# A spectral convolution loop regrouped: four turns a group, three PSUM bank pairs, split matrix halves

## The chip, the cores and the metric

The kernel runs on one core of a Trainium2 chip. The metric is the device time of one execution in microseconds (us). The kernel before has a median of 2602.63 us over three runs, from 2549.55 to 2603.58. All profile lines come from one profiled execution of 2596.2 us, whose span from first to last instruction is 2594.2 us.

## What is computed

Two layers act on x, four images of 56x56 positions with 128 channels, all in fp32. The first layer adds a 7x7 neighbourhood attention. The second adds a linear attention, and then a state-space layer (STU), which is the part that matters here:

```python
def _compute_spectral(u, sigma, phi, Mpp, Mpm):
    U_plus, U_minus = _stu_conv(phi, u, PADDED_SL)      # FFT convolution of u with 16 filters
    s = sigma ** SIGMA_POW
    out = jnp.einsum('btkd,k,kde->bte', U_plus, s, Mpp)
    out = out + jnp.einsum('btkd,k,kde->bte', U_minus, s, Mpm)
    return out

def _stu(u, sigma, phi, Mu, Mpp, Mpm):
    return _compute_spectral(u, sigma, phi, Mpp, Mpm) + _compute_ar_u(Mu, u)
...
for i, frac in enumerate((1, 2, 4, 8)):
    xi = x[:, :T // frac]
    si = _stu(xi, sigma, phi, M_u[i], M_phi_plus[i], M_phi_minus[i])
    outs.append(jnp.pad(si, ((0, 0), (0, T - si.shape[1]), (0, 0))))
y_soft = jax.nn.softmax((log_weights + gumbel) / TEMPERATURE)
y_hard = jax.nn.one_hot(jnp.argmax(y_soft), 4, dtype=y_soft.dtype)
weights = y_hard - jax.lax.stop_gradient(y_soft) + y_soft
return jnp.sum(jnp.stack(outs, axis=-1) * weights, axis=-1)
```

The convolutions are linear, so in frequency space each frequency has one complex 128x128 matrix, a sum over the 32 filters (16 plus, 16 minus), and the output there is that matrix times the transform of the tokens.

## The kernel before

**Stages.** A first stage selects and scales the filter matrices and transforms the filters (to about 100 us). Its `filter_matrices` (L277 on) sums the raw matrices with their weights into `to`, reorders them on GpSimd into `got` (L303), and brings them through DRAM to `mats`, which holds in each of four 32-partition strips one quarter of the output columns for the 32 filters. The main stage then runs both attentions image by image, to 1345 us. The spectral loop follows, to 2440 us. A last stage turns the result back into rows of the image, adds it, and writes the output.

**The spectral loop.** A frequency is m = m1 + 42 m2. The loop runs over 42 groups m1; each group has 56 points m2. Four kinds of work are done on TensorE for a group:

- `matrices` (L990) makes the 56 complex matrices of the group, 16 output columns of all of them in one call. It makes 16 matmuls, four columns by four strips, each with 32 rows, 128 columns of weights and 112 moving columns (56 points, two parts). They go to two PSUM tiles `pg` of two banks each. DVE copies the first tile and ACT the second to `gt` in SBUF (L1006). Eight calls make a group.
- `token_points` (L975) transforms the tokens of the group, one half of the image rows in one call, into the PSUM tile `pu`, from which DVE (L987) and ACT (L988) write `us`. `us` holds, for each point, 16 columns twice over: real and imaginary parts, and the negative imaginary part ahead of them, so that one slice serves each part of the complex product.
- `product` (L1011) multiplies one point: two matmuls, with 16 columns of `us` as weights and 128 columns of `gt` as moving data, that add up in PSUM. Point m2 writes 16 rows of one of the four 32-partition quadrants of `py`. After every 16 points `gather` (L1024) copies the used 16 rows of each quadrant to `ys`, two quadrants by ACT and two by DVE.
- `columns` (L1047) takes a group whose products have gone to DRAM and come back regrouped (`regroup`, L1033, `yd` to `yg`), transforms it along the points with two matmuls into `pz`, one tile of PSUM used twice, has ACT copy each to `zs` (L1059), and stores `zs` to `zd`.

Groups are pipelined: in step `it` the loop makes the matrices and token points of group `it`, the products of group `it`-1 and the columns of group `it`-3. TensorE's order is written out by hand (`manual_schedule` for PE, L1069). A step has eight turns. In each come one call of `matrices`, in turns 1 and 3 one of `token_points`, in turn 5 `columns`, and then seven points of `product`. The orders of the other engines are made by a scheduler.

**Buffers and waits.** [...] `pg` has two tags of one tile of two banks, so four banks and one buffer for each; `py` has two tiles of one bank; `pu` and `pz` one bank each. A tile's next user waits until the readers of its last content are done. When two engines read one PSUM tile, the framework also orders the second reader after the first. DMAs of the loop are issued on SyncE's queue: token loads `xm`, table loads `v`, `tok`, `back`, and `yd`, `yg`, `zd`.

Of the kernel before, what the change touches and what calls it, by code (L numbers as in the profile page):

```python
# [10 lines left out]
F32 = mybir.dt.float32  # L11
# [4 lines left out]
P = 128  # L16
B, H, W, C = 4, 56, 56, 128
# [33 lines left out]
NS, BR = 2, H // 2  # L51
N1, N2 = 42, W
NP = N1 * N2
NG = 4
# [3 lines left out]
NSB = NS * B  # L58
# [62 lines left out]
def hybrid_kernel(  # L121
# [23 lines left out]
    nc = tc.nc  # L145
# [17 lines left out]
    mats = keep.tile([P, GE, C], F32, name="mats")  # L163
# [15 lines left out]
    def evacuate(dst, src):  # L179

        flip[0] ^= 1
        if flip[0]:
            nc.scalar.copy(dst, src)
        else:
            nc.vector.tensor_copy(dst, src)
# [12 lines left out]
    with ExitStack() as ph:  # L198
# [78 lines left out]
        def filter_matrices():  # L277

            got = prep.tile([P, NG, GE, GE], F32, name="got")
            for c in range(4):  # L280
                cd = GE // 4
                to = prep2.tile([P, cd * C], F32, name="m_sum", bufs=1)
                for i in range(NE):
                    raw = prep2.tile([P, cd, C], F32, name="m_raw")
                    for s, m in enumerate((M_plus, M_minus)):
                        nc.sync.dma_start(
                            raw[64 * s : 64 * (s + 1)],
                            bass.AP(
                                m.tensor,
                                m.offset + (i * NF * C + c * cd) * C,  # L290
                                [[GE * C, NF * NG], [C, cd], [1, C]],
                            ),
                        )
                    src = raw.rearrange("p d e -> p (d e)")
                    if i == 0:
                        nc.vector.tensor_scalar(to, src, s_fac[:, 0:1], None, ALU.mult)
                    else:
                        nc.vector.scalar_tensor_tensor(
                            to, src, s_fac[:, i : i + 1], to, ALU.mult, ALU.add
                        )  # L300

                for g in range(NG):
                    nc.gpsimd.tensor_copy(  # L303
                        got[:, g, :, c * cd : (c + 1) * cd].rearrange("p (h i) d -> p h i d", i=4),
                        to.rearrange("p (d h g i) -> p g h i d", h=8, g=NG, i=4)[:, g],
                    )
            nc.sync.dma_start(wd, got.rearrange("p g e d -> p g (e d)"))
            for g in range(NG):
                for q in range(NG):
                    nc.sync.dma_start(  # L310
                        mats[32 * g : 32 * (g + 1), :, q * GE : (q + 1) * GE],
                        wd[:, g].rearrange("(k q) (e d) -> q k e d", q=NG, d=GE)[q],
                    )
# [60 lines left out]
    with main as ph:  # L374
# [552 lines left out]
        rows = iter(())  # L927
# [16 lines left out]
    with ExitStack() as ph:  # L944
        tabs = ph.enter_context(tc.tile_pool(name="tabs", bufs=2))
        sp = ph.enter_context(tc.tile_pool(name="sp", bufs=2))
        ps_g = ph.enter_context(tc.tile_pool(name="ps_g", bufs=1, space=bass.MemoryType.PSUM))
        ps_y = ph.enter_context(tc.tile_pool(name="ps_y", bufs=2, space=bass.MemoryType.PSUM))
        ps_x = ph.enter_context(tc.tile_pool(name="ps_x", bufs=1, space=bass.MemoryType.PSUM))

        chunk = {}

# [19 lines left out]
                nc.sync.dma_start(xm[part * N2 : (part + 1) * N2], xd[part * N1 + m1])  # L972
            return xm

        def token_points(m1, xm, us, s):  # L975

            pu = ps_x.tile([P, B, 2, N2], F32, tag="u", name="pu")
            for b in range(B):
                nc.tensor.matmul(  # L979
                    pu[:, b].rearrange("p c m -> p (c m)"),  # L980
                    xm[:, s, b, :],
                    tables_of(m1)[1],
                    start=True,
                    stop=True,
                )
            at = slice(s * B, (s + 1) * B)
            nc.vector.tensor_copy(us[:, 1:3, at, :], pu.rearrange("p b c m -> p c b m"))  # L987
            nc.scalar.mul(us[:, 0, at, :], pu[:, :, 1, :], -1.0)  # L988

        def matrices(m1, gt, eh):  # L990

            v = tables_of(m1)[0]
            pg = [ps_g.tile([P, 2, 512], F32, tag=f"g{q}", name=f"pg{q}") for q in range(2)]
            for i in range(4):
                for g in range(NG):
                    rows = slice(32 * g, 32 * (g + 1))
                    nc.tensor.matmul(  # L997
                        pg[g // 2][:, g % 2, 2 * N2 * i : 2 * N2 * (i + 1)],
                        mats[rows, 4 * eh + i, :],
                        v[rows],  # L1000
                        start=True,
                        stop=True,
                    )
            for q, copy in enumerate((nc.vector.tensor_copy, nc.scalar.copy)):
                e0 = 16 * eh + 8 * q
                copy(  # L1006
                    gt[:, :, e0 : e0 + 8, :].rearrange("p m (g i) c -> p g m i c", g=2),
                    pg[q][:, :, : 8 * N2].rearrange("p g (i m c) -> p g m i c", i=4, c=2),
                )

        def product(py, gt, us, m2):  # L1011

            j, slot = m2 % NG, m2 // NG % 4
            for c in range(2):

                nc.tensor.matmul(  # L1016
                    py[32 * j : 32 * j + 2 * NSB, slot, :],
                    us[:, 1 - c : 3 - c, :, m2],
                    gt[:, m2, :, c],
                    start=(c == 0),  # L1020
                    stop=(c == 1),
                )

        def gather(py, ys, q):  # L1024

            n = min(4, N2 // NG - 4 * q)
            for j in range(NG):
                rows = slice(32 * j, 32 * j + 2 * NSB)
                (nc.vector.tensor_copy if j % 2 else nc.scalar.copy)(  # L1029
                    ys[rows, 4 * q : 4 * q + n], py[rows, :n]  # L1030
                )

        def regroup(m1, ys):  # L1033
# [10 lines left out]
                )  # L1044
            return yg

        def columns(m1, yg):  # L1047

            zs = sp.tile([2 * N2, NS, B * C], F32, name="zs")
            for s in range(NS):  # L1050
                pz = ps_x.tile([2 * N2, B * C], F32, tag="z", name="pz")
                nc.tensor.matmul(  # L1052
                    pz,
                    tables_of(m1)[2],
                    yg[:, s * B : (s + 1) * B].rearrange("p k e -> p (k e)"),
                    start=True,
                    stop=True,
                )
                nc.scalar.copy(zs[:, s], pz)  # L1059
            for part in range(2):  # L1060
                nc.sync.dma_start(
                    zd[:, part * N1 + m1].rearrange("w s b e -> w (s b e)"),
                    zs[part * N2 : (part + 1) * N2].rearrange("w s f -> w (s f)"),
                )

        xms = {0: load_tokens(0)}
        gts, uss, ygs = {}, {}, {}
        LAG = 3
        with tc.manual_schedule(engines={mybir.EngineType.PE}):  # L1069
            for it in range(N1 + LAG):  # L1070
                ap = it - 1
                if it < N1:
                    gts[it] = sp.tile([P, N2, C, 2], F32, name="gt")
                    uss[it] = sp.tile([P, 3, NSB, N2], F32, name="us")
                    if it + 1 < N1:
                        xms[it + 1] = load_tokens(it + 1)
                if 0 <= ap < N1:
                    ys = sp.tile([P, N2 // NG, C], F32, name="ys")
                done = 0
                for eh in range(8):  # L1080
                    if it < N1:
                        matrices(it, gts[it], eh)
                        if eh in (1, 3):
                            token_points(it, xms[it], uss[it], eh // 2)
                    if eh == 5 and 0 <= it - LAG < N1:
                        columns(it - LAG, ygs.pop(it - LAG))
                    if 0 <= ap < N1:
                        for m2 in range(7 * eh, 7 * eh + 7):
                            if m2 % 16 == 0:
                                py = ps_y.tile([P, 4, C], F32, name="py")  # L1090
                            product(py, gts[ap], uss[ap], m2)
                            if m2 % 16 == 15 or m2 == N2 - 1:
                                gather(py, ys, m2 // 16)
                if 0 <= ap < N1:
                    ygs[ap] = regroup(ap, ys)
                xms.pop(it, None), gts.pop(ap, None), uss.pop(ap, None)


    with ExitStack() as ph:
# [91 lines left out]
```

## Time and profile before

| what | value |
|---|---|
| median of three runs | 2602.63 us |
| profiled execution, its span | 2596.2 us, 2594.2 us |
| mean granted TensorE clock | 0.791 |
| PE busy, of the span | 2149.8 us (83%) |
| DVE busy | 1348.2 us (52%) |
| ACT busy | 1077.8 us (42%) |
| first matmul of the spectral loop | 1350.0 us |
| last column product of the loop | 2438.8 us |

PE is TensorE's matmuls, PEld its weight loads, DVE is VectorE, ACT is ScalarE, POOL is GpSimd and SP is SyncE. In lines of the timeline come the start, the length, the engine, the line of the kernel, the operation, output<-inputs with their shapes, the number of instructions that were merged, and in brackets the engine's idle time before them and who ended it. An fp32 matmul leaves two records, so 16 matmuls show as x32. The granted clock is the share of TensorE's full speed that its throttle allowed.

### The profile page before, as it was taken

What the parts mean: (1) busy time and instruction counts of PE and PEld (TensorE: products, weight loads), DVE (VectorE), ACT (ScalarE), POOL (GpSimd) and SP (SyncE); (2) the same over time, 40 slices, a digit from 0 to 9 for tenths busy, and PEclk for the clock granted to TensorE, in tenths of its full rate; (3) what the DMA queues carried; (4) which work ended last, traced back from release to release, by engine and by line L of the source; (5) the groups of instructions that cost most, each with busy time, mean ns of one, the idle gap of its engine ahead of it and who ended that gap; (6) DMA issues with size and microseconds to landing.
All of it is one profiled execution on the core that took longest, in us unless ns stands there. A gap on an engine that the chain in (4) does not pass through costs nothing.

```text
span 2594.2 us, 66462 instructions
## 1 busy us (share of the span) xinstructions
PE 2149.8 (83%) x28564; PEld 1488.6 (57%) x28564; DVE 1348.2 (52%) x3324; ACT 1077.8 (42%) x2521; POOL 144.1 (6%) x287
## 2 busy tenths in 40 slices
PE   3069977898878987998868888888888888888498
PEld 3036655565645655665536766666676676666222
DVE  5246645464454645664425555556555555655132
ACT  0026542464334633564314555555555555555100
POOL 1110011001110002001000000000000000000000
PEclk8565588557975579656868999999999999999655
DMA  6631004011320113110351333433333343333597
GB/s 167 135 115 33 23 18 118 22 34 30 115 75 22 30 49 102 55 34 12 101 161 38 85 78 79 90 78 84 78 84 79 78 90 78 79 71 64 125 233 196
DMA packets 219512, 210.07 MB, mean 81 GB/s; under 512 B 43154, under 2 KB 187250, under 8 KB 218642
## 3 DMA queue, kind: packets, MB, share of 16 engines
q1 hardware_dynamic: 197850, 189.31, 29.2%
q10 hardware_dynamic: 21368, 16.51, 2.5%
q8 instruction: 224, 3.67, 0.6%
q14 instruction: 70, 0.57, 0.1%
HBM read 116.32 MB, written 89.45 MB: 79 GB/s over the span
## 4 chain that ended last, share of the span: by engine, by line
PE 56%; DVE 19%; ACT 10%; DMA 9%; issue 3%; POOL 1%; ACTq 1%; SPq 0%; DVEq 0%; POOLq 0%
PE pg L997 8%; PE pt L797 7%; PE sp L738 7%; DVE ys L1029 7%; PE py L1016 6%; ACT ys L1029 5%; DVE gt L1006 5%; PE po L819 4%; PE po L826 4%; ACT gt L1006 3%; PE bs L548 3%; PE pz L1052 2%; DMA out_dram<-tl 2%; PE pu L979 2%; PE po L1122 2%
## 5 line engine op out<-in xcount | busy, mean ns | idle before, releaser
L1006 DVE COPY gt<-pg 128x896 f32<-128x896 f32 x336 | 366.7, 1091 | 289.3 <-PE pg L997 278.1
L997 PE MATMUL pg<-v,mats 32*128 32x112 f32 x10752 | 398.0, 285 | 100.8 <-DVE gt L1006 83.9
L997 PEld LDWEIGHTS pg<-v,mats 32*128 32x128 f32 x10752 | 337.7, 190 | 190.1 <-DVE gt L1006 165.0
L1006 ACT COPY gt<-pg 128x896 f32<-128x896 f32 x336 | 304.5, 906 | 244.4 <-PE pg L997 232.4
L1016 PE MATMUL py<-gt,us 128*16 128x128 f32 x9408 | 389.8, 283 | 2.5 <-DVE gt L1006 1.6
L766 ACT ACTIVATE st<-st,nmx 96x252 f32<-96x252 f32 (+1 forms) x560 | 272.6, 488 | 190.5 <-DVE nmx L755 190.5
L1016 PEld LDWEIGHTS py<-gt,us 128*16 128x16 f32 x9408 | 295.0, 112 | 67.4 <-issue 31.1
L1029 DVE COPY ys<-py 16x512 f32<-16x512 f32 (+1 forms) x336 | 209.5, 624 | 160.3 <-ACT ys L1029 156.5
L755 DVE CUSTOM_DVE_ANT_0 st<-sp,relb 96x252 f32<-96x252 f32 (+1 forms) x560 | 203.5, 399 | 73.9 <-PE sp L738 73.5
L1029 ACT COPY ys<-py 16x512 f32<-16x512 f32 (+1 forms) x336 | 174.6, 520 | 149.3 <-DVE ys L1029 141.1
L738 PE MATMUL sp<-kp,qT 32*96 32x252 f32 (+1 forms) x1120 | 195.1, 635 | 30.4 <-DVE nmx L755 29.8
L797 PEld LDWEIGHTS pt<-ident,st 96*126 96x126 f32 (+1 forms) x1120 | 163.8, 216 | 87.4 <-issue 82.4
L797 PE MATMUL pt<-ident,st 96*126 96x96 f32 (+1 forms) x1120 | 201.5, 360 | 0.0
L1122 PE MATMUL po<-z,onto 84*56 84x512 f32 x224 | 125.8, 1066 | 21.1 <-DMA z<-zd 21.1
L1052 PE MATMUL pz<-yg,back 112*112 112x512 f32 x168 | 97.1, 660 | 46.7 <-ACT zs L1059 36.2
L597 ACT ACTIVATE hn<-acc,v 128x128 f32<-128x128 f32 (+1 forms) x208 | 83.0, 482 | 100.7 <-DVE v L588 99.4
L819 PE MATMUL po<-p,v_sb 126*32 126x96 f32 (+1 forms) x2240 | 115.1, 356 | 0.0
L738 PEld LDWEIGHTS sp<-kp,qT 32*96 32x96 f32 (+1 forms) x1120 | 67.3, 237 | 82.3 <-DVE nmx L755 58.4
L808 DVE COPY p<-pt 126x384 f32<-126x384 f32 (+1 forms) x140 | 74.1, 529 | 68.4 <-PE pt L797 64.0
L1131 DVE SCALAR_TENSOR_TENSOR tl<-po,hmask,tl 56x512 f32<-56x512 f32 x56 | 42.0, 750 | 124.3 <-PE po L1122 123.6
L766 ACT ACTIVATION_READ_ACCUMULATOR st<-st,nmx 96x1 f32 (+1 forms) x560 | 105.3, 188 | 0.0
L826 PE MATMUL po<-ident,wide 96*128 96x96 f32 x280 | 101.7, 465 | 0.0
(167 smaller groups left out, 2228.4 us busy)
## 6 DMA issues: line engine op xcount, KB each, us to landing
xd<-xs SPq DMA_DIRECT2D x112, 168.0 KB
xm<-xd SPq DMA_DIRECT2D x84, 224.0 KB
yd<-ys SPq DMA_DIRECT2D x168, 112.0 KB
yg<-yd SPq DMA_DIRECT2D x84, 224.0 KB
zd<-zs SPq DMA_DIRECT2D x84, 224.0 KB
z<-zd SPq DMA_DIRECT2D x14, 1344.0 KB
v_sb<-vpad SPq DMA_DIRECT2D x224, 63.0 KB
vpad<-vt SPq DMA_DIRECT2D x56, 112.0 KB
```

The source lines that it names most:

```text
L738: nc.tensor.matmul(t["sp"][h // 2][:nq, h % 2, : 2 * kn], qT[hs, ty, QR * x0 : QR * x0 + nq], kp[hs, y0 : y0 + KR, x0 : x0 + qc + KS - 1], ...
L755: nc.vector.tensor_tensor_reduce(st[:nq, h, : 2 * kn], t["sp"][h // 2][:nq, h % 2, : 2 * kn], relb[tiles[n][2]][:, h], -1.0, 3.0e38, ALU.a ...
L766: nc.scalar.activation(st[:nq, h, : 2 * kn], st[:nq, h, : 2 * kn], AF.Exp, bias=t["nmx"][:nq, h : h + 1], scale=-1.0, accum_out=t["sum"][: ...
L797: nc.tensor.transpose(pt[:kn, h, :nq], st[:nq, h, c * kn : (c + 1) * kn], ident[:nq, :nq])
L819: nc.tensor.matmul(po[hs, :nq], t["v"][:kn, c, hs], t["p"][c][:kn, h, :nq], start=(c == 0), stop=(c == 1),)
L826: nc.tensor.matmul(po[:, P : P + nq], t["wide"][:nq].rearrange("q h c -> q (h c)"), ident[:nq, :nq], start=True, stop=True,)
L997: nc.tensor.matmul(pg[g // 2][:, g % 2, 2 * N2 * i : 2 * N2 * (i + 1)], mats[rows, 4 * eh + i, :], v[rows], start=True, stop=True,)
L1006: copy(gt[:, :, e0 : e0 + 8, :].rearrange("p m (g i) c -> p g m i c", g=2), pg[q][:, :, : 8 * N2].rearrange("p g (i m c) -> p g m i c", i= ...
L1016: nc.tensor.matmul(py[32 * j : 32 * j + 2 * NSB, slot, :], us[:, 1 - c : 3 - c, :, m2], gt[:, m2, :, c], start=(c == 0), stop=(c == 1),)
L1029: (nc.vector.tensor_copy if j % 2 else nc.scalar.copy)(ys[rows, 4 * q : 4 * q + n], py[rows, :n])
L1052: nc.tensor.matmul(pz, tables_of(m1)[2], yg[:, s * B : (s + 1) * B].rearrange("p k e -> p (k e)"), start=True, stop=True,)
L1122: nc.tensor.matmul(po[64 * q : 64 * q + H].rearrange("p b c -> p (b c)"), onto[:, s], zin[q][:, i, s], start=(s == 0), stop=(s == NS - 1),)
```

## The change

The step keeps its work and its pipeline, and is divided otherwise.

- A step has four turns in place of eight. A turn makes two calls of `matrices`, then 16 points of `product` in a row (eight in the last turn), and one copy of the whole `py` tile to `ys`, by ACT and DVE in turn (`evacuate`). In the last turn both `token_points` and both `columns` stand between matrices and products.
- `ps_g` becomes one ring of three tiles of two banks. A call of `matrices` takes two of them. In each tile the first bank holds columns that DVE copies and the second columns that ACT copies, so four copies of 448 elements replace two of 896. `gt` is split in two halves of 64 columns, one written by each engine. `filter_matrices` orders the columns of `mats` to match.
- `py` has one bank. The token points and columns take their PSUM from one bank used twice (`x0`, `x1`) and from a tile of the ring (`xx`, a bank for each).
- `us` becomes two lasting tiles with two more blocks of 8 columns, zeroed once by GpSimd. A product's weights are then 32 columns wide, and fill the whole quadrant of `py`.
- The column products are copied by ACT and DVE in turn, each has its own PSUM, and their store is issued after `regroup`.

```diff
@@ filter_matrices
-                        got[:, g, :, c * cd : (c + 1) * cd].rearrange("p (h i) d -> p h i d", i=4),
-                        to.rearrange("p (d h g i) -> p g h i d", h=8, g=NG, i=4)[:, g],
+                        got[:, g, :, c * cd : (c + 1) * cd].rearrange("p (n i) d -> p n i d", i=4),
+                        to.rearrange("p (d h n q i) -> p q h n i d", h=2, n=8, q=2, i=4)[
+                            :, g // 2, g % 2
+                        ],
@@ pools
-        ps_g = ph.enter_context(tc.tile_pool(name="ps_g", bufs=1, space=bass.MemoryType.PSUM))
-        ps_y = ph.enter_context(tc.tile_pool(name="ps_y", bufs=2, space=bass.MemoryType.PSUM))
+        sp1 = ph.enter_context(tc.tile_pool(name="sp1", bufs=1))
+        ps_g = ph.enter_context(tc.tile_pool(name="ps_g", bufs=3, space=bass.MemoryType.PSUM))
+        ps_y = ph.enter_context(tc.tile_pool(name="ps_y", bufs=1, space=bass.MemoryType.PSUM))
...
+        us2 = [sp1.tile([P, 5, NSB, N2], F32, name=f"us{i}") for i in range(2)]
+        for t in us2:
+            nc.gpsimd.memset(t[:, 3:], 0.0)
@@ matrices
-            pg = [ps_g.tile([P, 2, 512], F32, tag=f"g{q}", name=f"pg{q}") for q in range(2)]
+            pg = [ps_g.tile([P, 2, 512], F32, tag="g", name="pg") for q in range(2)]
...
-            for q, copy in enumerate((nc.vector.tensor_copy, nc.scalar.copy)):
-                e0 = 16 * eh + 8 * q
-                copy(
-                    gt[:, :, e0 : e0 + 8, :].rearrange("p m (g i) c -> p g m i c", g=2),
-                    pg[q][:, :, : 8 * N2].rearrange("p g (i m c) -> p g m i c", i=4, c=2),
-                )
+            for q in range(2):
+                for h, copy in enumerate((nc.vector.tensor_copy, nc.scalar.copy)):
+                    e0 = 8 * n + 4 * q
+                    copy(
+                        gt[:, h, :, e0 : e0 + 4, :],
+                        pg[q][:, h, : 8 * N2].rearrange("p (i m c) -> p m i c", i=4, c=2),
+                    )
@@ product
-                    py[32 * j : 32 * j + 2 * NSB, slot, :],
-                    us[:, 1 - c : 3 - c, :, m2],
-                    gt[:, m2, :, c],
+                    py[32 * j : 32 * (j + 1), slot, :],
+                    us.rearrange("p c k m -> p (c k) m")[:, NSB * (1 - c) : NSB * (5 - c), m2],
+                    gt[:, :, m2, :, c],
@@ columns
-                pz = ps_x.tile([2 * N2, B * C], F32, tag="z", name="pz")
...
-                nc.scalar.copy(zs[:, s], pz)
+            evacuate(zs[:, s], pz)
@@ the loop
-                for eh in range(8):
+                for q in range(4):
                     if it < N1:
-                        matrices(it, gts[it], eh)
-                        if eh in (1, 3):
-                            token_points(it, xms[it], uss[it], eh // 2)
-                    if eh == 5 and 0 <= it - LAG < N1:
-                        columns(it - LAG, ygs.pop(it - LAG))
+                        matrices(it, gts[it], 2 * q)
+                        matrices(it, gts[it], 2 * q + 1)
+                    if q == 3:
+                        x0 = ps_x.tile([P, 512], F32, tag="x", name="px")
+                        xx = ps_g.tile([P, 2, 512], F32, tag="g", name="xx")
+                        x1 = ps_x.tile([P, 512], F32, tag="x", name="px")
+                        if it < N1:
+                            token_points(it, xms[it], us2[it % 2], 0, x0)
+                            token_points(it, xms[it], us2[it % 2], 1, xx[:, 0])
+                        if 0 <= az < N1:
+                            columns(az, ygs[az], zs, 0, xx[:, 1])
+                            columns(az, ygs[az], zs, 1, x1)
                     if 0 <= ap < N1:
-                        for m2 in range(7 * eh, 7 * eh + 7):
-                            if m2 % 16 == 0:
-                                py = ps_y.tile([P, 4, C], F32, name="py")
-                            product(py, gts[ap], uss[ap], m2)
-                            if m2 % 16 == 15 or m2 == N2 - 1:
-                                gather(py, ys, m2 // 16)
+                        n = min(16, N2 - 16 * q)
+                        py = ps_y.tile([P, 4, C], F32, name="py")
+                        for m2 in range(16 * q, 16 * q + n):
+                            product(py, gts[ap], us2[ap % 2], m2)
+                        evacuate(ys[:, 4 * q : 4 * q + n // NG], py[:, : n // NG])
                 if 0 <= ap < N1:
                     ygs[ap] = regroup(ap, ys)
+                if 0 <= az < N1:
+                    store_columns(az, zs)
+                    ygs.pop(az)
```

More of the change, by code (lines that the diff above doesn't have):

```diff
@@ L973, in load_tokens, with token_points @@
             return xm
-        def token_points(m1, xm, us, s):
-            pu = ps_x.tile([P, B, 2, N2], F32, tag="u", name="pu")
+        def token_points(m1, xm, us, s, pu):
+            pu = pu[:, : 2 * B * N2].rearrange("p (b c m) -> p b c m", b=B, c=2)
             for b in range(B):
@@ L988, in token_points, with matrices @@
             nc.scalar.mul(us[:, 0, at, :], pu[:, :, 1, :], -1.0)
-        def matrices(m1, gt, eh):
+        def matrices(m1, gt, n):
             v = tables_of(m1)[0]
-            pg = [ps_g.tile([P, 2, 512], F32, tag=f"g{q}", name=f"pg{q}") for q in range(2)]
+            pg = [ps_g.tile([P, 2, 512], F32, tag="g", name="pg") for q in range(2)]
             for i in range(4):
@@ L998, in matrices @@
                         pg[g // 2][:, g % 2, 2 * N2 * i : 2 * N2 * (i + 1)],
-                        mats[rows, 4 * eh + i, :],
+                        mats[rows, 4 * n + i, :],
                         v[rows],
@@ L1016, in product @@
                 nc.tensor.matmul(
-                    py[32 * j : 32 * j + 2 * NSB, slot, :],
-                    us[:, 1 - c : 3 - c, :, m2],
-                    gt[:, m2, :, c],
+                    py[32 * j : 32 * (j + 1), slot, :],
+                    us.rearrange("p c k m -> p (c k) m")[:, NSB * (1 - c) : NSB * (5 - c), m2],
+                    gt[:, :, m2, :, c],
                     start=(c == 0),
                     stop=(c == 1),
[L1022 to L1030, printed above, removed]
                 )
@@ L1045, in regroup, with columns, store_columns @@
             return yg
-        def columns(m1, yg):
-            zs = sp.tile([2 * N2, NS, B * C], F32, name="zs")
-            for s in range(NS):
-                pz = ps_x.tile([2 * N2, B * C], F32, tag="z", name="pz")
[L1052 to L1059, printed above, removed]
+        def columns(m1, yg, zs, s, pz):
+            pz = pz[: 2 * N2]
+            nc.tensor.matmul(
+                pz,
+                tables_of(m1)[2],
+                yg[:, s * B : (s + 1) * B].rearrange("p k e -> p (k e)"),
+                start=True,
+                stop=True,
+            )
+            evacuate(zs[:, s], pz)
+        def store_columns(m1, zs):
             for part in range(2):
@@ L1066, in hybrid_kernel @@
         xms = {0: load_tokens(0)}
-        gts, uss, ygs = {}, {}, {}
+        gts, ygs = {}, {}
         LAG = 3
@@ L1070, in hybrid_kernel @@
             for it in range(N1 + LAG):
-                ap = it - 1
+                ap, az = it - 1, it - LAG
                 if it < N1:
-                    gts[it] = sp.tile([P, N2, C, 2], F32, name="gt")
-                    uss[it] = sp.tile([P, 3, NSB, N2], F32, name="us")
+                    gts[it] = sp.tile([P, 2, N2, C // 2, 2], F32, name="gt")
                     if it + 1 < N1:
@@ L1078, in hybrid_kernel @@
                     ys = sp.tile([P, N2 // NG, C], F32, name="ys")
-                done = 0
-                for eh in range(8):
+                if 0 <= az < N1:
+                    zs = sp.tile([2 * N2, NS, B * C], F32, name="zs")
+                for q in range(4):
                     if it < N1:
-                        matrices(it, gts[it], eh)
-                        if eh in (1, 3):
-                            token_points(it, xms[it], uss[it], eh // 2)
-                    if eh == 5 and 0 <= it - LAG < N1:
-                        columns(it - LAG, ygs.pop(it - LAG))
-                    if 0 <= ap < N1:
-                        for m2 in range(7 * eh, 7 * eh + 7):
-                            if m2 % 16 == 0:
-                                py = ps_y.tile([P, 4, C], F32, name="py")
-                            product(py, gts[ap], uss[ap], m2)
-                            if m2 % 16 == 15 or m2 == N2 - 1:
-                                gather(py, ys, m2 // 16)
+                        matrices(it, gts[it], 2 * q)
[10 more added lines that the diff above has]
+                            columns(az, ygs[az], zs, 1, x1)
+                    if 0 <= ap < N1:
+                        n = min(16, N2 - 16 * q)
[3 more added lines that the diff above has]
+                        evacuate(ys[:, 4 * q : 4 * q + n // NG], py[:, : n // NG])
@@ L1094, in hybrid_kernel @@
                 if 0 <= ap < N1:
                     ygs[ap] = regroup(ap, ys)
-                xms.pop(it, None), gts.pop(ap, None), uss.pop(ap, None)
+                if 0 <= az < N1:
+                    store_columns(az, zs)
+                    ygs.pop(az)
+                xms.pop(it, None), gts.pop(ap, None)
     with ExitStack() as ph:
```

## The prediction

> **What bounds the kernel now.** I read the granted clock and the busy time by stretches first, to find the stage that the change touches. The spectral loop fills the middle of the page: its first matrices start at 1350 us and its last column product at 2438 us. Between 1400 and 2400 us each 200 us look alike, at clock 1.00:
>
> ```profile
> 1800.00:2000.00 200.00, 176.01 (x3967) 137.61 (x3964) 118.06 (x144) 102.31 (x160) 0.00 (x0) 1.00 0.36 81
> ```
>
> (stretch, then busy time and count of PE, PEld, DVE, ACT, POOL, then clock, DMA share, GB/s). PE is busy 88%, DVE 59%, ACT 51%, DMA a third: TensorE with its waits is the bound, and the copies matter where they make it wait. The waits in the loop say where:
>
> ```profile
> PEld pg L997 <- DVE gt L1006: 152.8, 240, 1.8
> DVE ys L1029 <- ACT ys L1029: 147.1, 278, 0.6
> PE pg L997 <- DVE gt L1006: 75.3, 121, 1.5
> PEld pz L1052 <- ACT zs L1059: 65.2, 38, 1.7
> ```
>
> (who waited for whom, us, times, longest). Matrices wait for the copy that frees their only pair of banks; that copy is late because it queues behind gathers of `ys`, which alternate between DVE and ACT, each waiting for the other. One group's length comes from the column products, one set a group: the first starts at 1441.4 us (group 3), the one of group 41 at 2398.16, so 956.76/38 = 25.18 us a group.
>
> The timeline inside a group gives the pieces (start, length, engine, line, work, idle before it and who ended it):
>
> ```profile
> 1807.59 1.15 PE L979 MATMUL pu<-tok,xm 112*128 112x112 f32 x8
> ...
> 1808.66 1.15 PE L1016 MATMUL py<-gt,us 128*16 128x128 f32 x28
> 1808.77 0.62 DVE L987 COPY us<-pu 128x448 f32<-128x448 f32 x1
> 1809.42 0.36 ACT L988 ACTIVATE us<-pu 128x224 f32<-128x224 f32 x1 [0.77 <-DVE us L987]
> ...
> 1809.74 1.16 PE L997 MATMUL pg<-v,mats 32*128 32x112 f32 x32
> ...
> 1810.83 1.17 PE L1016 MATMUL py<-gt,us 128*16 128x128 f32 x28
> 1810.94 1.09 DVE L1006 COPY gt<-pg 128x896 f32<-128x896 f32 x1 [1.55 <-PE pg L997]
> 1811.00 0.91 ACT L1006 COPY gt<-pg 128x896 f32<-128x896 f32 x1 [1.22 <-PE pg L997]
> ...
> 1812.08 0.98 PEld L997 LDWEIGHTS pg<-v,mats 32*128 32x128 f32 x32 [0.36 <-DVE gt L1006]
> ```
>
> Three readings. Matrices take 1.09 us from their start to the next work's start, and their copy starts 1.20 after their start. DVE ends a copy at 1812.03 and PE goes on at 1812.08: 0.05. And `us` shows what happens when both engines read one PSUM tile: ACT waits for DVE although another part is read, and starts 0.03 after it; the two copies of `gt`, from two tiles, run side by side.
>
> **What the Trainium skill says.** "PSUM — Partial Sum Buffer", Specifications: ScalarE and VectorE can read PSUM in parallel at full rate as long as they don't collide in a bank. The `gt` copies agree (1091 and 906 ns, together); so an order between them on two banks is the program's, not the chip's. "TensorEngine Tiling (Array Packing)", Key Properties: changing the tiling mode drains the array. Here 28 product records have their loads issued in 0.88 us, but 1.08 pass before the next matrices where nothing is waited for, so about 0.2 to 0.27 a switch. "TensorE: Matmul & The Clock Gate", Part 1: the clock falls after an idle window of some 3.4 us. No run shows that number by itself; the trace keeps 1.00 in stretches of 3.4 us with PE busy for only 1.9. Same page, LDWEIGHTS: the load's time goes with its columns. The trace bounds that for the wider weights, below.
>
> **The change, part by part**, with group times in us.
>
> *Gathers.* Per group 16 copies of 16 partitions (684 and 574 ns, the last four 417 and 356) become four copies of 128 partitions with the same length. About 9.0 us of alternating copies go, and 3x0.63+0.39, about 2.3, remain. None is on PE's path afterwards: each runs during the next turn's first matrices, which need 1.20 before their own copy can start. The price without that cover is 0.7 a turn.
>
> *Products.* `us` grows to 32 columns of weights for full quadrants. In the attention, loads of 126x32 have a shortest time of 106 ns and those of 128x16 a median of 108; I take no difference. Bounds: none below, since the moving columns stay the same; above, an estimate from the skill's price on that page (columns/1.2 ns): 16 more columns are 13 ns, over four quadrants 3.3 a record, 224 records 0.75 a group. The pace is read where products run in a row at the loop's end:
>
> ```profile
> 2408.46 4.04 PE L1016 MATMUL py<-gt,us 128*16 128x128 f32 x128 [1.58 <-DVE gt L1006]
> ```
>
> (4.04-0.27)/128 = 29.4 ns a record. Sixteen points are 64 records: 1.89+0.27 = 2.16; eight are 1.21.
>
> *Matrix copies.* This part decides. Each pair tile now holds one half for DVE and one for ACT. In the built program every ACT copy of `gt` waits for a DVE count only, none for PE: it follows the DVE copy of its own tile, as `us` does in the profile. PE in its turn waits for the ACT count of the copy that frees a pair. A copy has 448 elements: DVE 0.62 (the `us` row has that size), ACT between 0.36 for 256 and 0.57 for 512, so 0.52. Totals per group rise from 8x1.09 to 16x0.62 = 9.9 on DVE and from 7.2 to 8.3 on ACT, far from full.
>
> *The ring.* A turn writes four pair tiles from a ring of three: A takes a0, a1; B takes b0, b1; b1 lands on a0's buffer. PE is in order, so all of B but four records, and the 16 products queued behind B, wait for a0's copies. From A's start: 1.20 to DVE's start, 0.62, hand-over 0.03, ACT 0.52, back to PE 0.06: B resumes at 2.43. B's rest is 1.09-0.10 = 0.99: 3.42. Products 2.16: 5.58. The next turn's A finds its buffers free (b0's ACT copy ends about 4.7 us into the turn). So three turns are 16.74. Without the wait A and B would take about 1.9 of it; the stall costs 1.5 a turn.
>
> *Last turn.* 3.42, then both token points in a row: 16 records, 0.89+1.09 = 1.98: 5.40. The column product into `xx` waits for ACT's read of the other half of `xx` (its wait is on that count): 0.11+0.62+0.03+0.36+0.06 = 1.18: 6.58. Two columns, 0.86+1.05: 8.49 (the profile's 1.11 a pair, 0.25 of it drain, and 1.04 to the next products). Eight points: 9.70. Before, the second column product waited for ACT instead (0.88); its own tile now removes that.
>
> *Sum.* 16.74+9.70 = 26.44 against 25.18: +1.26 a group, 42 groups: +53. The first group, at half clock and without products, stalls as before but with its token points no longer filling waits: +4. The tail has one gather in place of four: about -4. Two memsets on POOL before the loop have no row here; their first reader is the products some 30 us later, so 0. The pool copies of the filter matrices keep their sizes: 0. DMAs keep sizes and count; on SP's queue a store of `zd` now stands between those of `yd`, with a whole group of slack. Against the profiled execution of 2596.2: 2649. The median of the runs shown is 6.4 above that: 2655, or +2.0%.
>
> **Rivals.** (1) *Copies side by side* (not slower). If the halves of a tile were read together, B would resume at 1.20+0.62+0.06 = 1.88, 0.55 earlier in each of four turns: 24.2 a group, -41 us, 2562. It decides at the hand-over in each tile: the loss is gone once a turn's stall shortens by 0.31. For it: different banks; against it: the waits as built, and `us` in this trace. The same place, smaller, gives no measurable change when the chain is shorter by some tenths. (2) *The stall hides wholly*, as three pairs might promise: 19.2 of PE's own work and the 1.18 of `us`: 20.4 a group, -200, 2400. Against it: PE is in order and no product stands between A and B. (3) *The clock falls*: an idle 1.3 in each turn lets the gate close at times. At half clock A, B and sixteen points take 2.1, 1.9 and 3.9, a turn 9.2 and a group some 44; one group in twenty at that pace adds 2.1x17.6 = 37, so 2692; a tenth 2729. For it: group 0 of the profile stays at 0.50 with PE busy 2.06 in 3.24 us. Against it: the loop holds 1.00 with 1.9 in 3.4, and a turn of the new loop has about 2.1 in its worst 3.4. (4) *Wider loads cost* 0.75 a group: +31, 2686.
>
> **Numbers.** Main case, with (4) as its upper edge: 0.84, a range of 2625 to 2686, which lies on both sides of the 2% line (2654.7) that is about what a measurement of this kernel can tell from no change. Side by side: 0.05. Hidden wholly: 0.03. Clock: 0.08. Runs of the kernel before go from 2549.55 to 2603.58, from a cause that this profile doesn't show; with a part of that below and the clock case above the range is 2605 to 2695. Slower by over 2%: half of the main case with the clock: 0.50. Within 2%: 0.47, the other half and the copies side by side. Faster: 0.03.
>
> **What would show it.** Right: a group of 26.4 us; PE waiting at matrices for ACT's `gt` about 1.3 us four times a group; DVE-to-ACT hand-overs on every `gt`; ACT copies of 0.52; products of 64 records in 2.16; `ys` off the list of waits; clock 1.00. Wrong: `gt` copies of one tile starting together, PE's wait at B under 1 us, product records over 31 ns, or a clock below 1.00 in the loop.

## The result and the profile after

The changed kernel takes 2677.4 us, median of four runs (2675.1 to 2679.69): slower, with a ratio of 1.0489 to the kernel before, interval 1.0463 to 1.0515. The forecast was slower, 2655 us, +2.0%. The profiled execution takes 2675.1 against 2596.2, which is 79 us or 3.0%. Of the 95 executions of all kernels here, seven, of four kernels, came some 50 us below the others of the same kernel, from a cause that no run shows, and the ratio above compares 2677 with two such executions of the kernel before (2549.55 and 2555.49). In the fifth experiment below the medians are 2677.13 to 2604.43, 1.028.

Ahead of the loop little moved: its first matrices start at 1351.1 us, before at 1350.0. From there to the last column product it is 1164.7 us, before 1088.8: +75.9. The stretch of the loop that the prediction showed, here from 1400 to 2400 us, of the changed kernel (busy time and count of PE, PEld, DVE, ACT, POOL, then clock, DMA share, GB/s):

```profile
1400.00:2400.00 1000.00, 798.45 (x18496) 678.55 (x18500) 454.15 (x776) 404.06 (x777) 0.00 (x0) 1.00 0.34 74
```

PE fell to 80% busy, DVE to 45%, ACT to 40%, the clock stayed at 1.00. Every engine waits more. The waits in the same stretch (us in total, times, longest):

```profile
ACT gt L1017 <- DVE gt L1017: 441.7, 297, 2.7
...
PEld pg L1007 <- ACT gt L1017: 187.8, 149, 1.6
PE pg L1007 <- ACT gt L1017: 161.4, 149, 1.4
...
PEld xx L1052 <- ACT us L997: 47.0, 35, 1.3
```

The waits of gathers for each other are gone. In their place ACT's copy of `gt` waits for DVE's, and matrices wait for ACT. The count is four a group, and the mean of one wait is 1.26 us (187.8/149), where a wait for DVE's copy took 0.64 before (152.8/240). One turn of the timeline:

```profile
1814.35 1.37 PE L1007 MATMUL pg<-v,mats 32*128 32x112 f32 x36
...
1815.54 1.16 DVE L1017 COPY gt<-pg 128x448 f32<-128x448 f32 x2 [2.36 <-PE pg L1007]
...
1816.20 1.06 ACT L1017 COPY gt<-pg 128x448 f32<-128x448 f32 x2 [1.16 <-DVE gt L1017]
...
1816.79 1.15 PE L1007 MATMUL pg<-v,mats 32*128 32x112 f32 x28 [1.07 <-ACT gt L1017]
...
1817.86 2.30 PE L1027 MATMUL py<-gt,us 128*32 128x128 f32 x64
...
1820.09 1.37 PE L1007 MATMUL pg<-v,mats 32*128 32x112 f32 x36
```

The first row is A's 32 records and four of B's, merged; then PE stands until ACT has finished the first of its two copies, 2.44 us after A's start. The turn takes 5.74. The last turn of a group has a second stall, between its token points and its columns:

```profile
1802.24 1.15 PE L988 MATMUL px<-tok,xm 112*128 112x112 f32 x8
...
1805.04 0.36 ACT L997 ACTIVATE us<-xx 128x224 f32<-128x224 f32 x1 [0.54 <-DVE us L996]
...
1805.45 1.11 PE L1052 MATMUL xx<-yg,back 112*112 112x512 f32 x2 [1.17 <-ACT us L997]
...
1807.35 1.25 PE L1027 MATMUL py<-gt,us 128*32 128x128 f32 x32
```

From the first token point to the products it takes 5.11 us, of which PE stands 1.17 until ACT has read the other half of `xx`. Column products show the group, `xx` at 1452.72 us and again at 2295.57, 31 groups later: 27.19 us in the mean (one of the 31 took 28.8, the others 27.1 to 27.2), before 25.18.

The products' weight loads before and after, and the copies of `ys` after, from the lists of groups (busy, mean ns of one, idle before and its releaser):

```profile
L1016 PEld LDWEIGHTS py<-gt,us 128*16 128x16 f32 x9408 | 295.0, 112 | 67.4 <-issue 31.1
...
L1027 PEld LDWEIGHTS py<-gt,us 128*32 128x32 f32 x9408 | 304.3, 144 | 47.5 <-issue 31.3
...
L185 DVE COPY ys<-py 128x512 f32<-128x512 f32 x84 | 46.9, 558 | 114.7 <-PE py L1027 109.3
```

A load of 32 columns takes 144 ns in the mean where the one of 16 took 112. The 558 ns of DVE's copies of `ys` is a mean over two sizes. No engine waits for a copy of `ys` in the stretch from 1400 to 2400 us any more.

### The profile page after: what moved, and what is told of

Its sections match the earlier page's. It is cut to its first block, busy times and chain, and to the rows that moved or that the text cites. A ratio compares the mean times of both kernels' runs of the same rounds, so it can differ in the third digit from the quotient of the medians.

```text
span 2673.4 us, 66713 instructions
## 1 busy us (share of the span) xinstructions
PE 2132.3 (80%) x28564; PEld 1533.1 (57%) x28564; DVE 1240.7 (46%) x3450; ACT 995.7 (37%) x2563; POOL 146.0 (5%) x289
## 4 chain that ended last, share of the span: by engine, by line
PE 72%; DVE 11%; DMA 7%; ACT 5%; issue 2%; POOL 1%; ACTq 1%; SPq 0%; DVEq 0%; POOLq 0%
PE pg L1007 14%; PE py L1027 12%; PE pt L799 7%; PE sp L740 7%; DVE gt L1017 4%; PE po L821 4%; ACT gt L1017 3%; PE po L828 3%; PE bs L550 3%; PE po L1133 2%; PE xx L1052 2%; PE px L988 2%; DMA z<-zd 2%; PE bs L883 1%; PE xx L988 1%
## 5 line engine op out<-in xcount | busy, mean ns | idle before, releaser
L1017 DVE COPY gt<-pg 128x448 f32<-128x448 f32 x672 | 388.3, 619 | 439.0 <-PE pg L1007 439.0
L1007 PE MATMUL pg<-v,mats 32*128 32x112 f32 x10752 | 432.0, 286 | 189.7 <-ACT gt L1017 183.6
L1017 ACT COPY gt<-pg 128x448 f32<-128x448 f32 x672 | 355.4, 533 | 510.8 <-DVE gt L1017 510.8
L1007 PEld LDWEIGHTS pg<-v,mats 32*128 32x128 f32 x10752 | 371.6, 190 | 251.8 <-ACT gt L1017 214.6
L1027 PE MATMUL py<-gt,us 128*32 128x128 f32 x9408 | 346.4, 291 | 2.1 <-DVE ys L185 1.3
L1027 PEld LDWEIGHTS py<-gt,us 128*32 128x32 f32 x9408 | 304.3, 144 | 47.5 <-issue 31.3
L1133 PE MATMUL po<-z,onto 84*56 84x512 f32 x224 | 126.9, 1067 | 21.8 <-DMA z<-zd 21.8
L185 DVE COPY ys<-py 128x512 f32<-128x512 f32 x84 | 46.9, 558 | 114.7 <-PE py L1027 109.3
L1133 PEld LDWEIGHTS po<-z,onto 84*56 84x56 f32 x224 | 32.5, 207 | 116.2 <-issue 101.0
L1052 PE MATMUL xx<-yg,back 112*112 112x512 f32 x84 | 48.5, 660 | 54.1 <-ACT us L997 45.5
```

Source lines behind the costliest of these rows:

```text
L1007: nc.tensor.matmul(pg[g // 2][:, g % 2, 2 * N2 * i : 2 * N2 * (i + 1)], mats[rows, 4 * n + i, :], v[rows], start=True, stop=True,)
L1017: copy(gt[:, h, :, e0 : e0 + 4, :], pg[q][:, h, : 8 * N2].rearrange("p (i m c) -> p m i c", i=4, c=2),)
L1027: nc.tensor.matmul(py[32 * j : 32 * (j + 1), slot, :], us.rearrange("p c k m -> p (c k) m")[:, NSB * (1 - c) : NSB * (5 - c), m2], gt[:, : ...
L1052: nc.tensor.matmul(pz, tables_of(m1)[2], yg[:, s * B : (s + 1) * B].rearrange("p k e -> p (k e)"), start=True, stop=True,)
L1133: nc.tensor.matmul(po[64 * q : 64 * q + H].rearrange("p b c -> p (b c)"), onto[:, s], zin[q][:, i, s], start=(s == 0), stop=(s == NS - 1),)
```

## The experiments

The theory is that two engines read each pair of banks one after the other, and that PE stands until the first pair is free again, because the fourth pair tile of a turn lands on its buffer. Its rivals are wider loads, the throughput of the copying engines, and a time that lies elsewhere in the kernel.

**The kernel before again.** No edit.

> The kernel before, unchanged, profiled a second time. The two profiled executions differ by 79 us (2596.2 to 2675.1), the compared runs by 4.9%, some 125 us: 46 us are not in the profile that the forecast was made from. Theory A: the loop of the kernel before can run at a shorter group than the 25.18 us of that profile (24.1 would give 46 us over 42 groups). Theory B: the time lies ahead of the loop, whose first matrices then start near 1305 us in place of 1350. If this execution takes 2596 again, it tells neither.

Measured: 2603.73 us over 18 runs (2598.26 to 2612.65); its profiled execution takes 2598.26 (2596.2 in the profile that the forecast started from), the first matrices start at 1354.6 us, and the group is 25.18 again. So that profile was a fair one. Neither theory is shown: none of the 18 executions came near 2552, and neither did any profiled one, so where those 50 us lie stays open.

**One tile for each copy.** The pair tile is cut into two tiles of one bank; each is read by one engine.

```diff
-        ps_g = ph.enter_context(tc.tile_pool(name="ps_g", bufs=3, space=bass.MemoryType.PSUM))
+        ps_g = ph.enter_context(tc.tile_pool(name="ps_g", bufs=6, space=bass.MemoryType.PSUM))
...
-            pg = [ps_g.tile([P, 2, 512], F32, tag="g", name="pg") for q in range(2)]
+            pg = [ps_g.tile([P, 512], F32, tag="g", name="pg") for g in range(NG)]
...
-                        pg[g // 2][:, g % 2, 2 * N2 * i : 2 * N2 * (i + 1)],
+                        pg[g][:, 2 * N2 * i : 2 * N2 * (i + 1)],
...
-                        pg[q][:, h, : 8 * N2].rearrange("p (i m c) -> p m i c", i=4, c=2),
+                        pg[2 * q + h][:, : 8 * N2].rearrange("p (i m c) -> p m i c", i=4, c=2),
...
-                        xx = ps_g.tile([P, 2, 512], F32, tag="g", name="xx")
+                        xx = [ps_g.tile([P, 512], F32, tag="g", name="xx") for h in range(2)]
...
```

> The changed kernel with a PSUM tile of one bank for each copy (a ring of six in place of three pairs), so that DVE's copy and ACT's copy of one call of matrices no longer read one tile. Theory (serial copies in the pair): PE resumes at matrices B 1.88 us after A's start in place of 2.44, 0.55 less in each of four turns, and the wait of the column product for ACT's read of us (1.2) goes with the split of xx: 27.1 - 2.2 - 1.2 = 23.7 us a group, about 2530 us. Rival (the copies' order costs nothing, PE waits for the engines' throughput): group stays within 0.5 of 27.1, 2655 to 2675.

Measured: 2520.4 us, median of four runs (2472.12 to 2525.05, three of them from 2518 on); the group is 23.42 (1469.27 to 2288.98 us, 35 groups). A turn of it:

```profile
1805.25 1.37 PE L1007 MATMUL pg<-v,mats 32*128 32x112 f32 x36
...
1806.43 1.16 DVE L1017 COPY gt<-pg 128x448 f32<-128x448 f32 x2 [2.33 <-PE pg L1007]
1806.47 0.97 ACT L1017 COPY gt<-pg 128x448 f32<-128x448 f32 x2 [0.52 <-PE pg L1007]
1807.11 0.97 PEld L1007 LDWEIGHTS pg<-v,mats 32*128 32x128 f32 x28 [0.66 <-DVE gt L1017]
```

The two engines copy side by side from two tiles, and PE resumes 1.86 us after A's start in place of 2.44. In the last turn the column product no longer waits for the read of `us`: from the first token point to the products it takes 3.69 us in place of 5.11. Four times 0.58 and once 1.42 are 3.74 of the 3.77 us by which the group is shorter. The time is gone where the theory puts it, and the order of the two readers is what made it: the copies are as many and as long as in the changed kernel (620 and 537 ns, there 619 and 533).

**Products between the two calls of matrices.** The pair tiles stay.

```diff
                         matrices(it, gts[it], 2 * q)
+                    if 0 <= ap < N1:
+                        n = min(16, N2 - 16 * q)
+                        py = ps_y.tile([P, 4, C], F32, name="py")
+                        for m2 in range(16 * q, 16 * q + 8):
+                            product(py, gts[ap], us2[ap % 2], m2)
+                    if it < N1:
                         matrices(it, gts[it], 2 * q + 1)
...
-                        for m2 in range(16 * q, 16 * q + n):
+                        for m2 in range(16 * q + 8, 16 * q + n):
                             product(py, gts[ap], us2[ap % 2], m2)
```

> The changed kernel with eight of a turn's sixteen products moved between its two calls of matrices; pair tiles and copies as they are. Theory (PE is in order and nothing stands between A and B): the 1.3 us wait at B is covered by 1.25 us of products; a turn is 1.09+1.25+1.09+1.25 and some 0.2 of waits at b1 and a1, 4.9 in place of 5.75, the last turn 8.5 in place of 9.8: 23.2 us a group, about 2510 us. Rival (the wider copies and loads are what costs): no more than 0.3 a group gained, about 2660.

Measured: 2503.65 us (2502.11 to 2506.84), ratio to the kernel before 0.9609, interval 0.9584 to 0.9634; group 23.00. From its waits and timeline:

```profile
PEld pg L1007 <- ACT gt L1017: 21.8, 111, 1.8
```

```profile
1814.76 1.15 DVE L1017 COPY gt<-pg 128x448 f32<-128x448 f32 x2 [1.25 <-PE pg L1007]
...
1815.47 1.01 ACT L1017 COPY gt<-pg 128x448 f32<-128x448 f32 x2 [1.17 <-DVE gt L1017]
1815.84 1.18 PEld L1007 LDWEIGHTS pg<-v,mats 32*128 32x128 f32 x32 [0.18 <-issue]
```

ACT still follows DVE in every tile, but PE's wait for it falls from 187.8 us (1400 to 2400 us) to 21.8 (1400 to 2300 us): it has products to do meanwhile. The same copies, as many and as wide, cost little with work over them. That excludes the throughput of the copying engines as what made the change slow.

**The gathers alone.** The kernel before with weights of 32 columns and one copy of `py`; turns, banks, `gt` and columns as before.

```diff
...
-                    py[32 * j : 32 * j + 2 * NSB, slot, :],
-                    us[:, 1 - c : 3 - c, :, m2],
+                    py[32 * j : 32 * (j + 1), slot, :],
+                    us.rearrange("p c k m -> p (c k) m")[:, NSB * (1 - c) : NSB * (5 - c), m2],
...
-            for j in range(NG):
-                rows = slice(32 * j, 32 * j + 2 * NSB)
-                (nc.vector.tensor_copy if j % 2 else nc.scalar.copy)(
-                    ys[rows, 4 * q : 4 * q + n], py[rows, :n]
-                )
+            evacuate(ys[:, 4 * q : 4 * q + n], py[:, :n])
```

> The kernel before with one part of the change alone: us of 32 columns, and one copy of 128 partitions for the four gathers of sixteen points; eight turns, banks, gt and column products as before. Theory (the gathers are what makes matrices wait in the kernel before): the group falls from 25.2 to about 23.5 us, 42 x 1.7 = 70 us below the kernel before on the same chip. Rival (the gathers lie beside TensorE's work and wider loads cost): within 15 us of the kernel before, or slower by the loads, 224 x 1.3 ns x 42 = 12 us.

Measured: 2530.11 us (2529.25 to 2535.63), ratio 0.9714, interval 0.9683 to 0.9746; group 23.50. The wait that led the list of the kernel before, with 152.8 us from 1400 to 2400 us, is here, from 1400 to 2300 us:

```profile
PEld pg L1001 <- DVE gt L1010: 53.8, 195, 0.3
```

So this part of the change, its wider loads included, is a gain of 75 us by itself, and the rest of it takes more than that back: 2677 against 2530.

**The changed kernel beside the kernel before.** No edit.

> The changed kernel unchanged, timed beside the kernel before on one chip. The group of 27.19 us in its profile against 25.18 gives 42 x 2.0 = 84 us. If that is the whole effect, the ratio to the kernel before is 1.028 to 1.032 on a chip where that takes 2605; if the first comparison's 1.049 is the change's own, some 2730.

Measured: 2677.13 us, median of four runs (2630.57 to 2680.07, three of them from 2674 on) against 2604.43 over seven runs (2600.72 to 2612.34), 1.028; group 27.17. The change costs 73 us from median to median.

**Columns ahead of token points.**

```diff
-                        if it < N1:
-                            token_points(it, xms[it], us2[it % 2], 0, x0)
-                            token_points(it, xms[it], us2[it % 2], 1, xx[:, 0])
                         if 0 <= az < N1:
-                            columns(az, ygs[az], zs, 0, xx[:, 1])
-                            columns(az, ygs[az], zs, 1, x1)
+                            columns(az, ygs[az], zs, 0, x0)
+                            columns(az, ygs[az], zs, 1, xx[:, 0])
+                        if it < N1:
+                            token_points(it, xms[it], us2[it % 2], 0, x1)
+                            token_points(it, xms[it], us2[it % 2], 1, xx[:, 1])
```

> The changed kernel with both column products ahead of both token points in the last turn, so that no column product writes a tile that ACT still has to read us from. Theory (that wait is 1.17 of the last turn and hidden by nothing): it goes, about 0.2 comes back as a token point waits for a copy of zs: 0.9 a group, 38 us, about 2637. Rival (the time is lost at the next wait, when us comes later): no more than 0.2 a group, 2668 to 2680.

Measured: 2628.55 us, median of four runs (2579.69 to 2630.53, three of them from 2627 on), 48.6 below the changed kernel, or 1.16 for each of 42 groups; the profile's group is 25.90. The last turn:

```profile
1817.04 1.11 PE L1052 MATMUL px<-yg,back 112*112 112x512 f32 x2
...
1818.19 0.69 DVE L185 COPY zs<-px 112x512 f32<-112x512 f32 x1
1818.93 0.97 PEld L988 LDWEIGHTS px<-tok,xm 112*128 112x128 f32 x8 [0.77 <-DVE zs L185]
...
1820.90 1.25 PE L1027 MATMUL py<-gt,us 128*32 128x128 f32 x32
```

From the first column product to the products it is 3.86 us, where the changed kernel has 5.11 from its first token point to them. The wait of 1.17 is gone whole: the copy of `zs` ends at 1818.88, as PE comes free, and little comes back. I had allowed 0.2 for that, which was too careful.

**Weights of 16 columns again.** One `py` tile, zeroed once, so that the unused rows of each quadrant can be copied.

```diff
+        py1 = ps_y.tile([P, 4, C], F32, name="py1")
+        nc.vector.memset(py1, 0.0)
...
-                    py[32 * j : 32 * (j + 1), slot, :],
-                    us.rearrange("p c k m -> p (c k) m")[:, NSB * (1 - c) : NSB * (5 - c), m2],
+                    py[32 * j : 32 * j + 2 * NSB, slot, :],
+                    us.rearrange("p c k m -> p (c k) m")[:, NSB * (1 - c) : NSB * (3 - c), m2],
...
-                        py = ps_y.tile([P, 4, C], F32, name="py")
+                        py = py1
```

> The changed kernel with product weights of 16 columns again, in a py tile zeroed once, everything else as changed. Theory A (wider loads set the pace): 64 product records take 2.16 us in place of 2.24, eight points 1.21 as before or less, together 0.3 to 0.8 a group: 13 to 34 us, 2643 to 2664. Theory B (the pace is that of the moving columns and of the longer row of products): products as now, 2675 to 2680.

Measured: 2652.25 us (2648.57 to 2655.43), 25 below the changed kernel, ratio to the kernel before 1.0178, interval 1.0158 to 1.0198; group 26.59. Sixteen points in its timeline:

```profile
1817.93 2.15 PE L1030 MATMUL py<-gt,us 128*16 128x128 f32 x64
...
1820.01 1.37 PE L1010 MATMUL pg<-v,mats 32*128 32x112 f32 x36
```

They take 2.08 us to the start of the next matrices, with wide weights 2.24; eight points take 1.11 and 1.19 (medians over the loop). The step from eight to sixteen is 32 records: 0.97/32 = 30 ns each with 16 columns, 1.05/32 = 33 with 32. Wider loads do set the pace a little, and cost 0.6 a group. They are not the main thing that makes the change slow: 2652 is still above 2604.

**Both repairs.** The edits of *One tile for each copy* and of *Products between the two calls of matrices*, together.

> Both repairs at once: a PSUM tile of one bank for each copy, and eight products between the two calls of matrices. If the two find the same stall from two sides, nothing waits at matrices any more: 8x1.09+7x1.18 and 3.7 for token points and columns are 20.7 us a group, 4.5 below the kernel before, about 2605-188 = 2417. If DVE (some 14 us a group) or the ring of banks then binds, 22 to 23 us a group, 2470 to 2510.

Measured: 2423.24 us (2418.79 to 2428.18), ratio 0.9302, interval 0.9277 to 0.9327; group 21.0 (1461.78 to 2217.66 us, 36 groups). From 1400 to 2200 us:

```profile
1400.00:2200.00 800.00, 795.20 (x19083) 665.07 (x19083) 467.11 (x803) 390.90 (x802) 0.00 (x0) 1.00 0.44 96
```

PE is busy 99%. The waits left at matrices are some 0.18 a change of work, which the profile puts partly on "issue". The two repairs together take 254 us off the changed kernel. Its layout was sound; what it lacked was a tile for each reader, and an order of work that gives PE something to do during the copies.

**Both repairs with weights of 16 columns.**

> Both repairs and product weights of 16 columns in a zeroed py tile. If narrower loads save here what they saved alone (25 us of the changed kernel) and TensorE sets the pace throughout: 2423-25 = 2398. If the copies have become what TensorE waits for, no more than 10 us: 2413 to 2423.

Measured: 2401.76 us (2395.19 to 2413.1) against 2603.8, 0.922. The gain of 21 is nearer to the 25 that the narrow weights gave alone than to 10, which fits a loop in which TensorE sets the pace. This is the best version here, 276 us below the changed kernel.

## Why the prediction was right or wrong

The direction and the mechanism were right; the size was not. The recorded ratio is some 125 us above its base (2677.4 against the mean, 2552.5, of the two executions that it compares with). Of these, 52 were forecast. The steps that failed make up the rest: terms of the sum that were mis-sized, above all *Products* and *the rest of B*, 22 us in all, and the base, 50 us. Term by term, in us of one group or turn:

| term | forecast | measured |
|---|---|---|
| A's start to B's resumption | 2.43 | 2.44, after a last turn 2.49 |
| rest of B | 0.99 | 1.07 |
| sixteen points | 2.16 | 2.24 |
| a turn | 5.58 | 5.82, 5.74, 5.74 |
| first token point to first column | 3.16 | 3.21 |
| two columns | 1.91 | 1.90 |
| eight points | 1.21 | 1.18 |
| last turn | 9.70 | 9.80 |
| a group | 26.44 | 27.10 by these terms, 27.19 in the mean |

*The ring* holds to 0.01 us in three of four turns: the chain of DVE, ACT and back to PE was read from the rows of the kernel before, and it is what the trace shows. Splitting the tiles and moving products shows it from two sides.

*Matrix copies* holds: 620 and 533 ns, 0.62 and 0.52 forecast.

*Products* failed. The prediction put the wider loads at nothing, because loads of 126x32 in the attention had a shortest time of 106 ns, beside a median of 108 for the narrow ones. That set a shortest time against a median: in this stream the median went from 108 to 140 ns. Its own upper bound, an estimate from the price in "TensorE: Matmul & The Clock Gate" (LDWEIGHTS) of the Trainium skill, was 3.3 ns a record; the runs show 33-30 = 3, and a record over 31 ns was on its list of signs of being wrong. With 16 columns the sixteen points take 2.08, so the wider loads cost 0.16, and the forecast of 2.16, made for loads that cost nothing, was itself 0.08 too long. Half of the error was covered by luck. The narrow weights give back 25 us.

*Rest of B* failed by 0.08 in each of four turns, 13 us: the prediction took off the whole 0.10 of the four records that are issued before the wait, and they save only 0.02.

*Last turn* holds but for 0.10, most of it the rest of B, and the wait for `us` is shown by columns ahead of token points.

*Gathers* holds: no one waits for `ys`. But their own gain, which the prediction left inside the sum of the group, is 75 us when it comes alone.

*Sum*: the ends of the loop give back some 8 us (75.9 in the loop against 42 x 2.01 = 84), where +4 and -4 were put down.

*The base* failed too. The median of the runs shown (2602.63) agrees with the later medians of 2603.73 to 2605.09, over 7 to 23 runs, and 1.028 is the change's effect against it. But the prediction put the execution of 2549.55 into its range alone and not into the base, while the recorded ratio has 2549.55 and 2555.49 as its base. Those 50 us stay unexplained; nothing in the mechanism of the prediction is about them.

The rivals: copies side by side, a stall that hides and a falling clock are all excluded by the trace of after. Wider loads that cost, the fourth, came true at nearly its price: +31 was put down, and narrow weights give back 25. Side by side was put at -41 us, and the split tiles give -84; they also free the columns, which the prediction's 1.18 a group makes 50 us more, together -91.

## What to carry to other kernels

Where the framework orders the readers of a tile, two engines that share one PSUM tile take turns even when each reads its own bank (2677 us here, 2520 with the tiles split): give each reader a tile of its own. A ring of buffers hides a copy only if its user has other work between its turns, so count what stands in PE's order between filling a buffer and needing the next. And when a change has several parts, run them alone: here one part gains 75 us, and the stall that the rest brings hides it.

## What the runs showed that was not expected

Column-tiled products with weights of 32 columns run at 33 ns a record and with 16 columns at 30, although the moving data is the same and the profile shows the loads during the matmuls. The "TensorE: Matmul & The Clock Gate" page of the Trainium skill prices loads by their columns (LDWEIGHTS). The difference of 3 ns agrees with the estimate of 3.3 that spreads that price over four quadrants. That it adds to the pace of this stream was not expected.

The clock stayed at 1.00 with PE idle a fifth of the time, in stalls of mostly 1.1 to 1.2 us. In the attention of the kernel before, from 1100 to 1200 us, it was 0.51 although the records of PE cover all of the 100 us. So the busy share of PE did not tell the clock here, and what did is not shown.
